# A graph network's last group of edges: nine columns instead of fourteen, and one pacing wait fewer

## The chip, the cores and the metric

The kernel runs on one core of a Trainium2 chip. The metric is the device time of one execution in microseconds (us). The core has five engines that work side by side, each with its own queue of instructions: TensorE (PE in the profile; PEld is its weight load), VectorE (DVE), ScalarE (ACT), GpSimd (POOL) and SyncE (SP). [...]data comes from device memory by DMA. The timed runs of the kernel before have a median of 8327.35 us (three runs, 8295.38 to 8355.8).

## The reference

There are 12500 nodes with 256 features each and 200000 edges, sorted by their destination node. Three graph layers are followed by one attention layer:

```
for each of three layers:                       # relu after the first two
    agg  = segment_sum(h[src], dst)             # sum over the incoming edges
    h    = h @ W_self + (agg / degree) @ W_neigh + b
x = layernorm(x + h)

zu = x @ U                                      # 4 heads of 16 numbers per node
logit = (zu[src] * zu[dst]).sum(-1) / 4         # per edge and head
alpha = softmax of logit over the edges of one destination
agg   = segment_sum(alpha * zu[src], dst)
half  = 0.5 * x + 0.5 * (head-weighted agg @ U^T)
x     = layernorm(x + relu(half + 0.5 * (half - half D^T D) D - 0.05))
```

Only the attention layer, the second block, is touched by the change at its heart. The matrices behind `half` are folded into two constants beforehand (`gz`, `gu`), so that per node only two products remain.

## The kernel before, in words

**Groups of edges.** The edges are cut into groups of `GE` = 128 x 14 = 1792. In a group, partition p holds 14 consecutive edges (`GT` = 14), one to a column. There are `NG` = 112 groups, numbered 0 to 111; the last has only 200000 - 111 x 1792 = 1088 edges. Laid fourteen to a partition they fill 77 partitions and 10 places of the next; what is left of the last group's 1792 places holds the destination `PAD` and the source 0. Because the edges are sorted, a group's destinations lie in a window of at most 128 nodes, that starts at the group's first destination (`starts`), or at node 12372 for the last groups, so that the window stays inside the table. `rel` is an edge's destination counted from the start of its group's window; a padded place lies far outside of it. All this is made once at the start (lines 187 to 279), from `srcI` and `dstI`, which are loaded at lines 198 to 202: all groups but the last by one transfer, the last by two more, on the queues of SP (dst) and ScalarE (src). The three layers (`fast_sage`) work through the groups up to a cut and do the remaining nodes in another way, so the last group is gathered in the attention alone.

**The attention** (`fast_attention`) takes the groups in turn. For each group:

1. SP loads rows of the window's 128 nodes, and `rel_d`, one row of 128 numbers per column, spread over all partitions (line 983), from which ScalarE makes `ohT`, a one-hot matrix from nodes to edges (lines 994 and 995).
2. GpSimd gathers the source rows of `zu_d` into `zs`, one indirect transfer of 128 rows per column, fourteen per group (lines 986 to 992, recorded at the helper's line 120).
3. VectorE makes `oh`, the one-hot matrix from edges to nodes (line 458).
4. In two halves of seven columns (`H` = 7), TensorE spreads the destination rows over the edges (`pD`, line 1006), VectorE multiplies by the gathered rows and sums (`zz`, `lg`, lines 1014 and 1017), ScalarE takes the exponential (1020) and copies it into the PSUM tile (1022), and both make the weighted rows `w` as a high and a low part (`wf`, `w`, lines 1023 to 1027).
5. TensorE sums `w` over the edges by node (`pA`, line 1030), with a product more that carries the sums of the group before into the new window (`carry`, line 465).
6. The sums are made into means (`acc`, `den`, `ag`, lines 1040 and 385 to 388), turned (`pT`, line 1044), multiplied (`pO`, lines 377 and 378), normalized (lines 402 to 403 and 333 to 338) and stored by SP (436).

**The order of the work.** `group` is a generator with five stages, and a loop starts one group and moves the four groups before it on by a stage. TensorE's order is written out: `in_order` chains every product to the one before it. In a round it has `pD` of group g, `pO` of g-3, `pT` of g-2 and `pA` of g-1. On the other engines a scheduler sets the order when the program is built, and each engine then works its queue off from the front. Two waits pace the gathers (`hold_back`): the first gather of a group waits for the products `pD` of the group before, and the eighth (`j == H`) waits for the sums `pA` of the group two before:

```
if j == 0 and g:
    hold_back(shown[-1], i)
if j == H and g > 1:
    hold_back(summed[g - 2], i)
```

Of the kernel before, what the change touches and what calls it, by code (L numbers as in the profile page):

```python
# [9 lines left out]
F32 = mybir.dt.float32  # L10
F32R = mybir.dt.float32r
# [5 lines left out]
AF = mybir.ActivationFunctionType  # L17
OP = mybir.AluOpType
# [5 lines left out]
P = 128  # L24
NB = 125
TE = 125
GT = 14
GE = P * GT
# [4 lines left out]
ND = 32  # L33
NDL = (16, 32, 32)
SG0, SG = 4, 8
# [13 lines left out]
def tile_gnn_resnorm(  # L49
# [13 lines left out]
    nc = tc.nc  # L63
    N, D = x.shape
    E = src.shape[0]
    K, _, R = u.shape
    KR = K * R
    DC = D // P
    NBLK = N // NB
    NG = -(-E // GE)  # L70
    L = len(w_self)
    AW = KR + K
    N0 = N - ND * P
# [4 lines left out]
    NU = ND // SG0  # L78
    U0 = NU - NDL[0] // SG0
# [18 lines left out]
            self.GS = (E * (self.n0 - P) // N - SLACK) // GE + 1  # L98
    cuts = {nd: Cut(nd) for nd in NDL}
    assert NQ % CB == 0 and NQ % ZB == 0 and NC * NQ < 512 and N0 % NC == 0 and SL == P == SG0 * P // NC  # L100
    assert NDL[0] % SG0 == 0 and 0 < U0 < NU and L == len(NDL) == 3 and NDL[1] == NDL[2] == ND and ND % SG == 0
    assert all(0 < c.GS < c.NGS < NG for c in cuts.values())
    assert N % NB == 0 and E % TE == 0 and D == 2 * P and KR == 64 and N + P < PAD and L > 1

# [10 lines left out]
    rel_d = dram.tile([NG * GT, P], F32, name="rel_d")  # L115
# [27 lines left out]
    npidx = const.tile([P, 1], F32, name="npidx")  # L143
# [43 lines left out]
    with tc.tile_pool(name="prep", bufs=1) as prep, \  # L187
# [3 lines left out]
        nc.vector.memset(dstI[:, NG - 1], PAD)  # L191
        nc.vector.memset(srcI[:, NG - 1], 0)
        last = (NG - 1) * GE
        full, rest = divmod(E - last, GT)
        EC = E // TE
        dall = prep.tile([TE, EC + SL], I32, name="dall")
        nc.vector.memset(dall[:, EC:], PAD)
        for t, ap, q in ((dstI, dst, nc.sync), (srcI, src, nc.scalar)):
            q.dma_start(t[:, :NG - 1], ap[:last].rearrange("(g p j) -> p g j", p=P, j=GT))
            q.dma_start(t[:full, NG - 1], ap[last:last + full * GT].rearrange("(p j) -> p j", j=GT))  # L200
            if rest:
                q.dma_start(t[full:full + 1, NG - 1, :rest], ap[E - rest:][None, :])
        nc.sync.dma_start(dall[:, :EC], dst.rearrange("(p j) -> p j", p=TE))
# [248 lines left out]
        nc.vector.tensor_copy(c, iota[:, :n])  # L452
        return c

    def onehot(wk, nodes, r, dt=F32, name="oh", op=OP.is_equal, bufs=2):

        oh = wk.tile([P, GT, P], dt, name=name, bufs=bufs)
        nc.vector.tensor_tensor(oh, r.unsqueeze(2).to_broadcast([P, GT, P]),  # L458
                                nodes.unsqueeze(1).to_broadcast([P, GT, P]), op=op)
        return oh  # L460

    def carry(wk, pa, d, before):
# [496 lines left out]
    def fast_attention():  # L959
        loads[0] = None  # L960
        H = GT // 2
        with tc.tile_pool(name="att", bufs=2) as wk, \
                tc.tile_pool(name="att_c", bufs=1, space=PSUM) as cps, \
                tc.tile_pool(name="att_ps", bufs=1, space=PSUM) as ps:
            nodes = group_consts(cps)
            order, sums = [None], [None]
            shown, summed = [], []

            def in_order(first, last):
                if order[0] is not None:  # L970
                    after(order[0], first)
                order[0] = last

            def group(g):

                zb = wk.tile([P, D], F32, name="zb", bufs=8)
                zT = wk.tile([P, DC, P], F32, name="zT", bufs=6)
                zn = wk.tile([P, KR], F32, name="zn", bufs=3)
                load_rows([(zn, zu_d), (zb, z_d), (zT, zt_d)], g)

                ohT = wk.tile([P, GT, P], F32R, name="ohT", bufs=3)
                rT = ohT.bitcast(F32).rearrange("p j e -> p (j e)")
                nc.sync.dma_start(rT, rel_d[g * GT:(g + 1) * GT, :].rearrange("j e -> (j e)")[None, :]
                                  .to_broadcast([P, GT * P]))
                zs = wk.tile([P, GT, KR], F32, name="zs", bufs=6)
                for j in range(GT):
                    i = gather(zs[:, j], zu_d, srcI[:, g, j:j + 1])

                    if j == 0 and g:
                        hold_back(shown[-1], i)  # L990
                    if j == H and g > 1:
                        hold_back(summed[g - 2], i)
                oh = onehot(wk, nodes, rel[:, g], F32R, bufs=3)
                nc.scalar.activation(ohT.rearrange("p j e -> p (j e)"), rT, AF.Abs, bias=npidx)
                nc.scalar.activation(ohT.rearrange("p j e -> p (j e)"), rT, AF.Relu, scale=-1.0, bias=1.0)

                z2 = wk.tile([P, K, 2, R], F32R, name="z2", bufs=3)
                zk = zn.rearrange("p (k r) -> p k r", r=R)
                nc.scalar.activation(z2[:, :, 0], zk, AF.Copy)
                nc.vector.tensor_tensor(z2[:, :, 1], zk, z2.bitcast(F32)[:, :, 0], op=OP.subtract)  # L1000

                w = wk.tile([P, GT, 2 * AW], F32R, name="w", bufs=3)
                for a in (0, H):

                    pd = ps.tile([P, (H + 1) * 2 * KR], F32, name="pD", bufs=2)
                    mm = [nc.tensor.matmul(pd[:, j * 2 * KR:(j + 1) * 2 * KR], ohT[:, a + j],  # L1006
                                           z2.rearrange("p k i r -> p (k i r)"), start=True, stop=True)
                          for j in range(H)]
                    in_order(mm[0], mm[-1])
                    shown.append(mm[-1])  # L1010

                    zg = zs[:, a:a + H].rearrange("p t (k r) -> p (t k) r", r=R)
                    zz = wk.tile([P, H * K, 2, R], F32, name="zz")
                    nc.vector.tensor_mul(zz, zg.unsqueeze(2).to_broadcast([P, H * K, 2, R]),  # L1014
                                         pd[:, :H * 2 * KR].rearrange("p (m i r) -> p m i r", i=2, r=R))
                    lg = wk.tile([P, H, K], F32, name="lg")
                    nc.vector.reduce_sum(lg.rearrange("p t k -> p (t k)"), zz.rearrange("p m i r -> p m (i r)"),  # L1017
                                         axis=AX.X)
                    wf = wk.tile([P, H, AW], F32, name="wf")
                    nc.scalar.activation(wf[:, :, KR:], lg, AF.Exp, scale=0.25)  # L1020
                    pe = pd[:, H * 2 * KR:H * (2 * KR + K)].rearrange("p (t k) -> p t k", k=K)
                    nc.scalar.activation(pe, wf[:, :, KR:], AF.Copy)
                    nc.vector.tensor_mul(wf[:, :, :KR].rearrange("p t (k r) -> p t k r", r=R),  # L1023
                                         zs[:, a:a + H].rearrange("p t (k r) -> p t k r", r=R),
                                         pe.unsqueeze(3).to_broadcast([P, H, K, R]))
                    nc.scalar.activation(w[:, a:a + H, :AW], wf, AF.Copy)
                    nc.vector.tensor_tensor(w[:, a:a + H, AW:], wf, w.bitcast(F32)[:, a:a + H, :AW], op=OP.subtract)  # L1027
                yield
                pa = ps.tile([P, 2 * AW], F32, name="pA")
                mm = [nc.tensor.matmul(pa, oh[:, j], w[:, j], start=j == 0, stop=g == 0 and j == GT - 1)  # L1030
                      for j in range(GT)]
                if g:
                    mm.append(carry(wk, pa[:, :AW], delta[:, g:g + 1], sums[0]))
                in_order(mm[0], mm[-1])
                summed.append(mm[-1])
                yield
                part = wk.tile([P, AW], F32, name="part")
                nc.scalar.activation(part, pa[:, AW:2 * AW], AF.Copy)
                acc = wk.tile([P, AW], F32, name="acc", bufs=3)
                nc.vector.tensor_add(acc, part, pa[:, :AW])  # L1040
                sums[0] = acc
                ag = attention_mean(wk, acc, 1e-30, OP.max)
                pt = ps.tile([P, P], F32, name="pT")
                mm = nc.tensor.transpose(pt[:KR], ag, ident)  # L1044
                in_order(mm, mm)
                yield
                agT = attention_turned(wk, pt, P)
                pg, *mm = gradient_step(ps, zT, agT)
                in_order(*mm)
                yield  # L1050
                o, made = attention_end(wk, zb, pg)
                store_rows([(o, out)], g, made)
                yield

            live = []
            for g in range(NG + 4):
                if g < NG:
                    live.append(group(g))  # L1060
                    next(live[-1])
                old = live[:-1] if g < NG else live
                for s in old:
                    next(s)
                if g >= 4:
                    live.pop(0)
            assert not live
# [204 lines left out]
```

## Time and profile before

| what | us |
|---|---|
| timed runs: median (lowest, highest) | 8327.35 (8295.38, 8355.8) |
| the profiled execution, as timed | 6588.12 |
| its span, from the first to the last instruction | 6586.3 |
| TensorE busy (share of the span) | 5115.1 (78%) |
| GpSimd busy | 4862.9 (74%) |
| VectorE busy | 3948.0 (60%) |
| ScalarE busy | 3431.3 (52%) |
| gathers of `zs` in the attention: 1568, busy | 1504.8 |
| mean granted clock of TensorE | 0.810 |

The profile is of one execution, and all its durations belong to that one, whose time stands in the second row; the timed runs are longer. A line of the page's groups names the source line, the engine, the tile written and the tiles read, and the count; then the busy time and the mean duration of one, and the idle time of the engine just before, with what ended it. In a listing in order of time the first number is the start, the second the duration, and the bracket at the end says how long the engine had been idle and what released it. The chain that ended last is followed back from the last instruction, at each step to what released it.

### The profile page before, as it was taken

The page shows a single profiled execution, that of the slowest core. Times are in us where ns is not written, and L with a number is a line of the kernel's source. Part 1 is how long each engine was busy: PE and PEld are TensorE (multiplying, and loading weights), DVE is VectorE, ACT ScalarE, POOL GpSimd, SP SyncE. Part 2 cuts the span into 40 slices and gives each one's busy share as a digit, 9 for nine tenths or more (in the row PEclk, how much of TensorE's full clock was granted, in tenths as well). Part 3 has the DMA queues.
Part 4 walks back from the last instruction along what each step waited for, and adds up shares of the span by engine and source line. Part 5 has one row for each costly group of instructions (what it writes and reads, how often), then busy time and mean ns, then how long its engine had stood idle before and what let it go on. Part 6 is the DMA issues. An engine that isn't in the chain of part 4 may idle for free. (4 is left out here: it accounts for less than half of the span.)

```text
span 6586.3 us, 86342 instructions
## 1 busy us (share of the span) xinstructions
PE 5115.1 (78%) x23316; PEld 4174.4 (63%) x23316; DVE 3948.0 (60%) x10037; ACT 3431.3 (52%) x6215; POOL 4862.9 (74%) x5038
## 2 busy tenths in 40 slices
PE   5778888788799999998899999995455555555555
PEld 3566666677577777776678888884444444444444
DVE  5778776455454555555556666666566555556655
ACT  2434444555466666665456666663455545545554
POOL 6767777777677777777677777774777777777775
PEclk8889999899899999999999999997555555555555
DMA  8967777888677888886788888884333333333332
GB/s 231 319 214 254 259 239 265 269 297 294 210 248 254 272 263 270 265 270 211 230 253 264 269 269 270 267 261 128 98 100 101 106 101 100 103 105 100 101 107 66
DMA packets 878807, 1367.35 MB, mean 208 GB/s; under 512 B 191090, under 2 KB 533130, under 8 KB 874207
## 3 DMA queue, kind: packets, MB, share of 16 engines
q1 hardware_dynamic: 629744, 802.71, 36.6%
q0 software_dynamic: 216000, 504.16, 25.6%
q10 hardware_dynamic: 32559, 54.81, 2.5%
q8 instruction: 187, 3.06, 0.2%
q14 instruction: 317, 2.60, 0.1%
HBM read 1150.87 MB, written 210.33 MB: 207 GB/s over the span
## 5 line engine op out<-in xcount | busy, mean ns | idle before, releaser
L120 POOL DMA_INDIRECT xg<-h_d,srcI x2128 | 2067.9, 972 | 696.5 <-issue 304.2
L750 PE MATMUL px<-c,hz 128*128 128x512 f32 x7840 | 2153.6, 414 | 102.3 <-ACT c L744 73.0
L120 POOL DMA_INDIRECT zs<-zu_d,srcI x1568 | 1504.8, 960 | 547.8 <-issue 434.3
L750 PEld LDWEIGHTS px<-c,hz 128*128 128x128 f32 x7840 | 1457.5, 192 | 402.0 <-ACT c L744 90.7
L120 POOL DMA_INDIRECT xg<-in_x_dram,srcI x1274 | 1228.7, 964 | 429.7 <-issue 159.0
L744 ACT ACTIVATE c<-c 128x1024 fp32r<-128x1024 uint8 (+1 forms) x1176 | 1063.0, 914 | 696.2 <-PE px L750 548.5
L850 DVE TENSOR_TENSOR hl<-xg,hl 128x256 fp32r<-128x256 f32 x2128 | 790.5, 420 | 529.3 <-ACT hl L848 506.6
L458 DVE TENSOR_TENSOR oh<-rel,gconst 128x1792 fp32r<-128x1792 f32 (+1 forms) x358 | 722.7, 2019 | 364.2 <-PE pA L856 228.1
L848 ACT ACTIVATE hl<-xg 128x512 fp32r<-128x512 f32 x1216 | 646.3, 571 | 529.1 <-DMA xg<-h_d,srcI 399.7
L1044 PE MATMUL pT<-ident,ag 128*64 128x128 f32 x112 | 47.3, 422 | 894.4 <-DVE ag L388 894.4
L1044 PEld LDWEIGHTS pT<-ident,ag 128*64 128x64 f32 x112 | 14.5, 129 | 974.2 <-DVE ag L388 972.2
L1014 DVE TENSOR_TENSOR zz<-zs,pD 128x896 f32<-128x896 f32 x224 | 242.8, 1084 | 637.5 <-DMA zs<-zu_d,srcI 633.5
L856 PE MATMUL pA<-hl,oh 128*128 128x512 f32 x2128 | 583.0, 409 | 10.9 <-DVE hl L850 8.1
L864 PE MATMUL pA<-xg,oh 128*128 128x258 f32 x1764 | 457.9, 410 | 21.4 <-DMA xg<-in_x_dram,srcI 16.8
L856 PEld LDWEIGHTS pA<-hl,oh 128*128 128x128 f32 x2128 | 406.8, 193 | 106.6 <-DVE hl L850 13.5
L641 ACT ACTIVATE win<-pc 128x392 uint16<-128x392 f32 x512 | 242.0, 500 | 359.6 <-PE pc L638 335.0
L864 PEld LDWEIGHTS pA<-xg,oh 128*128 128x128 f32 x1764 | 350.2, 206 | 90.9 <-DMA xg<-in_x_dram,srcI 26.2
L1006 PE MATMUL pD<-z,ohT 128*128 128x128 f32 x1568 | 361.8, 418 | 38.5 <-DVE wf L1023 20.1
L1006 PEld LDWEIGHTS pD<-z,ohT 128*128 128x128 f32 x1568 | 348.0, 334 | 39.2 <-DVE wf L1023 20.5
L1030 PE MATMUL pA<-w,oh 128*128 128x136 f32 x1568 | 362.3, 419 | 0.0
L1020 ACT ACTIVATE wf<-lg 128x28 f32<-128x28 f32 x224 | 50.6, 226 | 583.0 <-DVE lg L1017 581.8
L630 DVE TENSOR_SCALAR ob<-iota,kt 128x196 bf16<-128x196 f16 x1024 | 349.3, 344 | 0.0
(254 smaller groups left out, 8002.1 us busy)
## 6 DMA issues: line engine op xcount, KB each, us to landing
hz<-hs_d SPq DMA_DIRECT2D x588, 512.0 KB
c<-cnt_d SPq DMA_DIRECT2D x112, 896.0 KB
ohT<-rel_d SPq DMA_DIRECT2D x112, 896.0 KB
hs_d<-hs SPq DMA_DIRECT2D x218, 256.0 KB
cnt_d<-win ACTq DMA_DIRECT2D x32, 1568.0 KB
xg<-h_d,srcI POOLq DMA_INDIRECT x2128
c<-cnt_d SPq DMA_DIRECT2D x56, 448.0 KB
zs<-zu_d,srcI POOLq DMA_INDIRECT x1568
```

What stands on the lines that cost most here:

```text
L120: return nc.gpsimd.indirect_dma_start(out=dst_ap, out_offset=None, in_=table, in_offset=bass.IndirectOffsetOnAxis(ap=idx, axis=0))
L458: nc.vector.tensor_tensor(oh, r.unsqueeze(2).to_broadcast([P, GT, P]), nodes.unsqueeze(1).to_broadcast([P, GT, P]), op=op)
L630: nc.vector.tensor_scalar(ob[:, c], iota16[:, 1:1 + NQ * 2], kt[:, 1, at], kt[:, 2, at], op0=OP.is_equal, op1=OP.mult)
L744: nc.scalar.activation(c32.rearrange("p (k d) -> p k d", d=P), c8[:, :, b % CB], AF.Copy)
L750: made.append(nc.tensor.matmul(px[f][i], hz[:, b % ZB, a:a + P].bitcast(F32R), c32[:, i * 512:(i + 1) * 512], start=b == 0 and part == 0, ...
L848: nc.scalar.activation(hi[:, b + j:b + j + n, :W], xg[:, a + j:a + j + n, :W], AF.Copy)
L850: nc.vector.tensor_tensor(lo[:, b + j, :D], xg[:, a + j, :D], hf[:, b + j, :D], op=OP.subtract)
L856: mm.append(nc.tensor.matmul(pa, oh[:, a + j], hl[:, j].rearrange("p i d -> p (i d)"), start=first, stop=stop))
L864: mm.append(nc.tensor.matmul(pa[:, :W], oh[:, a + j], xg[:, a + j, :W], start=first, stop=stop))
L1006: mm = [nc.tensor.matmul(pd[:, j * 2 * KR:(j + 1) * 2 * KR], ohT[:, a + j], z2.rearrange("p k i r -> p (k i r)"), start=True, stop=True) f ...
L1014: nc.vector.tensor_mul(zz, zg.unsqueeze(2).to_broadcast([P, H * K, 2, R]), pd[:, :H * 2 * KR].rearrange("p (m i r) -> p m i r", i=2, r=R))
L1030: mm = [nc.tensor.matmul(pa, oh[:, j], w[:, j], start=j == 0, stop=g == 0 and j == GT - 1) for j in range(GT)]
```

## The change

For the last group alone, the edges are laid nine to a partition: `LT` is the number of columns that 1088 edges need over 128 partitions, which is 9. They fill 120 partitions and 8 places of the next. Everything that the attention does per column is done for `T` columns, where `T` is 14, and 9 for the last group: nine gathers, a one-hot matrix of nine columns on either side, halves of seven and two columns, nine products `pD` and nine `pA`. The arrays keep their sizes; the columns 9 to 13 of the last group hold padding. The eighth gather of the last group (`j == H`) is no longer held back; that of all other groups is, as before. Cut to its core:

```
+    LT = -(-(E - (NG - 1) * GE) // P)
...
-        full, rest = divmod(E - last, GT)
+        full, rest = divmod(E - last, LT)
...
-            q.dma_start(t[:full, NG - 1], ap[last:last + full * GT].rearrange("(p j) -> p j", j=GT))
+            q.dma_start(t[:full, NG - 1, :LT], ap[last:last + full * LT].rearrange("(p j) -> p j", j=LT))
...
-    def onehot(wk, nodes, r, dt=F32, name="oh", op=OP.is_equal, bufs=2):
+    def onehot(wk, nodes, r, dt=F32, name="oh", op=OP.is_equal, bufs=2, m=GT):
...
-        nc.vector.tensor_tensor(oh, r.unsqueeze(2).to_broadcast([P, GT, P]),
-                                nodes.unsqueeze(1).to_broadcast([P, GT, P]), op=op)
+        nc.vector.tensor_tensor(oh[:, :m], r[:, :m].unsqueeze(2).to_broadcast([P, m, P]),
+                                nodes.unsqueeze(1).to_broadcast([P, m, P]), op=op)
...
+                T = GT if g < NG - 1 else LT
...
-                rT = ohT.bitcast(F32).rearrange("p j e -> p (j e)")
-                nc.sync.dma_start(rT, rel_d[g * GT:(g + 1) * GT, :].rearrange("j e -> (j e)")[None, :]
-                                  .to_broadcast([P, GT * P]))
+                rT = ohT.bitcast(F32)[:, :T].rearrange("p j e -> p (j e)")
+                nc.sync.dma_start(rT, rel_d[g * GT:g * GT + T, :].rearrange("j e -> (j e)")[None, :]
+                                  .to_broadcast([P, T * P]))
...
-                for j in range(GT):
+                for j in range(T):
...
-                    if j == H and g > 1:
+                    if j == H and 1 < g < NG - 1:
                         hold_back(summed[g - 2], i)
-                oh = onehot(wk, nodes, rel[:, g], F32R, bufs=3)
+                oh = onehot(wk, nodes, rel[:, g], F32R, bufs=3, m=T)
...
-                for a in (0, H):
+                for a, n in ((0, H), (H, T - H)):
...
-                mm = [nc.tensor.matmul(pa, oh[:, j], w[:, j], start=j == 0, stop=g == 0 and j == GT - 1)
-                      for j in range(GT)]
+                mm = [nc.tensor.matmul(pa, oh[:, j], w[:, j], start=j == 0, stop=g == 0 and j == T - 1)
+                      for j in range(T)]
```

Within a half, every operation on `H` columns becomes one on `n` columns: `zz`, `lg`, `wf`, the copy into the PSUM tile, and both parts of `w`.

More of the change, by code (lines that the diff above doesn't have):

```diff
@@ L100, in tile_gnn_resnorm @@
     assert NQ % CB == 0 and NQ % ZB == 0 and NC * NQ < 512 and N0 % NC == 0 and SL == P == SG0 * P // NC
-    assert NDL[0] % SG0 == 0 and 0 < U0 < NU and L == len(NDL) == 3 and NDL[1] == NDL[2] == ND and ND % SG == 0
+    assert NDL[0] % SG0 == 0 and 0 < U0 < NU and L == len(NDL) == 3 and NDL[1] == NDL[2] == ND and ND % SG == 0 and GT // 2 < LT <= GT
     assert all(0 < c.GS < c.NGS < NG for c in cuts.values())
@@ L990, in group @@
                         hold_back(shown[-1], i)
-                    if j == H and g > 1:
+                    if j == H and 1 < g < NG - 1:
                         hold_back(summed[g - 2], i)
-                oh = onehot(wk, nodes, rel[:, g], F32R, bufs=3)
-                nc.scalar.activation(ohT.rearrange("p j e -> p (j e)"), rT, AF.Abs, bias=npidx)
-                nc.scalar.activation(ohT.rearrange("p j e -> p (j e)"), rT, AF.Relu, scale=-1.0, bias=1.0)
+                oh = onehot(wk, nodes, rel[:, g], F32R, bufs=3, m=T)
+                oT = ohT[:, :T].rearrange("p j e -> p (j e)")
+                nc.scalar.activation(oT, rT, AF.Abs, bias=npidx)
+                nc.scalar.activation(oT, rT, AF.Relu, scale=-1.0, bias=1.0)
                 z2 = wk.tile([P, K, 2, R], F32R, name="z2", bufs=3)
@@ L1007, in group @@
                                            z2.rearrange("p k i r -> p (k i r)"), start=True, stop=True)
-                          for j in range(H)]
+                          for j in range(n)]
                     in_order(mm[0], mm[-1])
                     shown.append(mm[-1])
[L1012 to L1015, printed above, removed]
@@ L1016, in group @@
-                    lg = wk.tile([P, H, K], F32, name="lg")
+                    zg = zs[:, a:a + n].rearrange("p t (k r) -> p (t k) r", r=R)
+                    zz = wk.tile([P, H * K, 2, R], F32, name="zz")[:, :n * K]
+                    nc.vector.tensor_mul(zz, zg.unsqueeze(2).to_broadcast([P, n * K, 2, R]),
+                                         pd[:, :n * 2 * KR].rearrange("p (m i r) -> p m i r", i=2, r=R))
+                    lg = wk.tile([P, H, K], F32, name="lg")[:, :n]
                     nc.vector.reduce_sum(lg.rearrange("p t k -> p (t k)"), zz.rearrange("p m i r -> p m (i r)"),
@@ L1018, in group @@
                                          axis=AX.X)
-                    wf = wk.tile([P, H, AW], F32, name="wf")
+                    wf = wk.tile([P, H, AW], F32, name="wf")[:, :n]
                     nc.scalar.activation(wf[:, :, KR:], lg, AF.Exp, scale=0.25)
-                    pe = pd[:, H * 2 * KR:H * (2 * KR + K)].rearrange("p (t k) -> p t k", k=K)
+                    pe = pd[:, H * 2 * KR:H * 2 * KR + n * K].rearrange("p (t k) -> p t k", k=K)
                     nc.scalar.activation(pe, wf[:, :, KR:], AF.Copy)
@@ L1023, in group @@
                     nc.vector.tensor_mul(wf[:, :, :KR].rearrange("p t (k r) -> p t k r", r=R),
[L1024 to L1027, printed above, removed]
+                                         zs[:, a:a + n].rearrange("p t (k r) -> p t k r", r=R),
@@ L1028, in group @@
+                                         pe.unsqueeze(3).to_broadcast([P, n, K, R]))
+                    nc.scalar.activation(w[:, a:a + n, :AW], wf, AF.Copy)
+                    nc.vector.tensor_tensor(w[:, a:a + n, AW:], wf, w.bitcast(F32)[:, a:a + n, :AW], op=OP.subtract)
                 yield
                 pa = ps.tile([P, 2 * AW], F32, name="pA")
-                mm = [nc.tensor.matmul(pa, oh[:, j], w[:, j], start=j == 0, stop=g == 0 and j == GT - 1)
-                      for j in range(GT)]
+                mm = [nc.tensor.matmul(pa, oh[:, j], w[:, j], start=j == 0, stop=g == 0 and j == T - 1)
+                      for j in range(T)]
```

## The prediction

> **What bounds the kernel now.** I read the page's busy times and slices first, then the groups of the attention stage, then the chain that ended last over the final 65 us, and last the instructions in order of time there.
>
> ```profile
> PE 5115.1 (78%) x23316; PEld 4174.4 (63%) x23316; DVE 3948.0 (60%) x10037; ACT 3431.3 (52%) x6215; POOL 4862.9 (74%) x5038
> ...
> POOL 6767777777677777777677777774777777777775
> PEclk8889999899899999999999999997555555555555
> ```
>
> The first line is the whole kernel, and settles nothing: two stages share it, as the clock in the last line shows. The busy times by stretch give the split: the layers run to about 4440 us with TensorE 77% to 95% busy, the attention takes the last 2146 us. There GpSimd is the steady engine, as its group of gathers between 5000 and 6480 us shows (busy us, mean ns, idle us before them):
>
> ```profile
> L120 POOL DMA_INDIRECT zs<-zu_d,srcI x1170 | 1124.5, 961 | 356.6 <-issue 323.7 <-DMA zs<-zu_d,srcI 32.3 <-PE pO L378 0.6
> ```
>
> That is 1.27 us from start to start, hardly ever held by anything but issue, and fourteen make a round of 17.7 us. So the stage goes at the pace of the gathers, and only its end can go differently.
>
> The chain that ended last (start, us, what), its end:
>
> ```profile
> 6543.94 2.40 DMA zs<-zu_d,srcI
> 6546.52 1.09 DVE zz L1014
> ...
> 6547.87 0.99 DVE lg L1017
> ...
> 6551.73 0.42 PE pT L1044
> 6552.15 2.89 PE pA L1030 x14
> 6555.03 0.43 PE pA L465 x2
> 6555.46 2.98 PE pD L1006 x14
> ...
> 6561.40 0.35 PE pT L1044
> ...
> 6568.38 2.89 PE pA L1030 x14
> ...
> 6580.64 0.41 DVE g L338
> ```
>
> One gather, issued at 6543.94, sets zz, and through VectorE's queue the mean ag and its transpose pT; from 6551.73 TensorE runs almost without a gap to the last products. The gathers there, in order of time:
>
> ```profile
> 6542.70 0.94 POOL L120 DMA_INDIRECT zs<-zu_d,srcI  x1 [0.30 <-issue]
> 6543.94 0.94 POOL L120 DMA_INDIRECT zs<-zu_d,srcI  x1 [0.30 <-PE pO L378]
> 6545.19 0.95 POOL L120 DMA_INDIRECT zs<-zu_d,srcI  x1 [0.30 <-issue]
> 6555.73 0.94 POOL L120 DMA_INDIRECT zs<-zu_d,srcI  x1 [9.59 <-PE pA L465]
> ```
>
> Here the built program's order is needed. The scheduler doesn't leave a held gather in its place: GpSimd's queue has the twelve unheld gathers of group g, then the eighth of group g-1, then the first of g. So the twelve of group 111 (the last) start from 6528.71 to 6542.70; 6543.94 is the eighth of group 110; 6545.19 is the first of 111; and 6555.73, after 9.59 us, is the eighth of 111, held by the sums of group 109. VectorE beside it:
>
> ```profile
> 6546.52 1.09 DVE L1014 TENSOR_TENSOR zz<-zs,pD 128x896 f32<-128x896 f32 x1 [4.89 <-DMA zs<-zu_d,srcI]
> 6551.45 0.22 DVE L388 TENSOR_TENSOR ag<-acc,den 128x64 f32<-128x64 f32 x1
> ...
> 6558.11 1.09 DVE L1017 TENSOR_REDUCE lg<-zz 128x28 f32<-128x896 f32 x1
> 6559.11 1.08 DVE L1014 TENSOR_TENSOR zz<-zs,pD 128x896 f32<-128x896 f32 x1
> ```
>
> zz of 110's second half waits 4.89 us for the gather of 6543.94. zz of 111's second half (6559.11) shows no idle at all: the gather that waited 9.59 us is not late for anyone.
>
> [...]0.94 us on GpSimd, but 2.40 us in the chain before zz may go. [...]The trace has the 1283 ns[...] (a load at 6541.71 has its exponential at 6543.00). [...]
>
> **The change part by part.** On every engine the program is the same up to the last rounds of the attention, apart from four loads at the start.
>
> *The loads (L200, L202).* 120 pieces of 36 bytes instead of 77 of 56, in each of two queues. The issue of L200 on SP shows 20.98 us behind L199's 14208 pieces, some 1.5 ns each: 43 more are 0.06 us. Above, a whole microsecond could be lost if short pieces cost 20 times that; below, nothing, since there are more pieces. VectorE first needs dstI at 26.76 us, while GpSimd gathers without pause from 3.85. I take 0. Without that cover it is 0.06 to 1 us. SP's later dall loads, queued behind, move by the same.
>
> *Five gathers fewer.* The last group issues nine. Eight (seven, and the eighth gather, now unheld) stand ahead of 110's eighth instead of twelve: 4 x 1.25 = 5.0 us, so it starts at 6538.95. Its own hold, the sums of 108, is over at 6537.87 (the carry L465 of that round starts at 6537.24), so the slot is kept, with 1.1 us to spare. It lands 2.4 us later, 6541.4. The first gather of 111 follows at 6540.20, or at 6541.1 once the products pD of 110 (to 6540.85) are done; needed near 6549, it has cover.
>
> *VectorE's queue before it.* oh of 111 starts at 6537.48 and has 1152 instead of 1792 elements: 1.36 for 2.02 us, to 6538.84. acc and sh (0.5 us) now go first, then 110's first zz at 6539.4, which needs seven pD products (6537.87 + 1.49 = 6539.36), and its reduction from 6540.6. So 110's second zz starts at 6541.6, for 6546.52.
>
> *ag moves up.* In the new order ag of 108 follows directly on the second reduction; before, it stood behind two wf and two w. zz 6541.6, reduction 6542.8, ag 6543.8 to 6544.0, where it ended at 6551.67: **7.6 us sooner**. TensorE is done with pO at 6543.82, so pT and pA of 109 follow at once; w of 109 has long been there. That ends the cover: next late is TensorE.
>
> *TensorE's share.* The last group's pD are nine, not fourteen: 5 x 2.98/14 = **1.1 us** less; pA likewise 5 x 2.89/14 = **1.0 us**. Both lie in the unbroken stretch.
>
> *A new wait.* pD of 111 ends at 6549.85, pO of 108 at 6552.8, and pT of 109 could go. But ag of 109 now stands in VectorE's queue behind g of 108 (L403), which waits for the Relu after that pO (0.55 us later in the trace: 6561.40 to 6561.95), and behind bn_st. So 6553.35 + 0.42 + 0.17 + 0.43 + 0.22 = 6554.6: **1.8 us** lost, with pA of 110 and everything behind pT on TensorE waiting. Bounds: 0, if the two engines overlap otherwise, to 3.
>
> *ScalarE.* The square-root table load now comes between the exponentials of 111 and their copies. Relu 6552.85, loads and exponentials to 6556.35, bn_rs and copies to 6557.0, wf, w on both engines to 6559.1. pT of 110 is due 6.6 us after pT of 109, 6561.2, and pA of 111 after it: 2.1 us of cover. I take 0[...]. The Abs on ohT (1.24 for 1.77 us) and the shorter zz, lg, wf, w lie beside TensorE's stretch: 0, at most 1 gained.
>
> *The pacing wait itself.* 0: its gather was late for nobody.
>
> Sum: -7.6 - 1.1 + 1.8 - 1.0 = **-7.9 us**. The profiled execution took 6588.1 us (6586.3 of span and 1.8 around it), so 6580.2. The three timed runs lie at 8327.35, 1.264 times that. Nothing in the profile says where those 1739 us lie. If none is in the tail, the gain is 7.9; if all stretches grow alike, 10.0. I take 9.3: **8318 us**.
>
> **The rivals.**
> *The cut stays hidden.* If ScalarE or the old order binds, the 7.6 are lost, and 2.1 remain: 8325. For it, VectorE has little room between 6539 and 6544; against it, the 4.89 us idle that names the gather. 0.14.
> *The wait was what held.* A reader of the waits would add its 9.59 us to five gathers of 1.25: 15.8 us, 8310. Against it stands zz at 6559.11 without idle. With it goes the case that the new wait of 1.8 us doesn't come (-9.7). 0.16.
> *Slower[...].* The place is the table load ahead of the copies of 111. It decides once the stretch from Relu to w takes over 2.1 us more, and ends above the old time once it takes 2.1 + 7.9 = 10 us more, 5 for each of its two table loads. At 12 more it is +2: 8329. The trace's 1283 ns speaks against it. 0.04.
> The forecast itself, a gain of 6 to 9 us in the profile: 0.66.
>
> **How the numbers follow.** All four lie within 0.2% of each other; a measurement of this kernel tells about 1% (83 us) from no change. The times shown spread 60 us over three runs, more than any case moves, so scatter makes the range. The rivals' gains on the lowest run give 8280 and on the highest 8357; three runs understate a spread, and both medians carry it, so I add 15 us on each side, rounded: 8265 to 8372. Over 1% either way needs scatter beyond anything shown: 0.05 faster, 0.04 slower, 0.91 within.
>
> **What would show it.** In the profile after: 110's second zz near 6541.6 with little or no idle; pT of 108 near 6544.1; no GpSimd wait near 10 us; pT of 109 with about 1.8 us of idle before it, released by ag; a span near 6578. If that idle is missing, the new wait was wrong; if zz still waits 4 us or more, the queue's order was. A change of over 20 us in the span would mean that something before the last rounds moved, and the whole reading would be wrong.

## The result, and the profile after

The kernel after takes 8339.38 us (median of 22 runs, 8287.14 to 8394.53), the kernel before, measured beside it, 8347.15 us (22 runs, 8276.94 to 8391.6). The ratio of after to before is put at 1.0004, with a 95% interval of 0.9985 to 1.0024 (the two medians alone give 0.9991): no difference that can be told. The interval is some 33 us wide, four times the 7.9 us that the working arrived at, so this number alone neither confirms nor refutes a single step, and every rival of the prediction would have passed by it too.

The profile can, with one caution. All timed runs of both kernels took 8205 to 8395 us, and so did the profiled execution of after (8334.37 us); the one profile of before that the prediction was made from, 6588.1 us, was of a shorter kind of execution that was not met again. For a fair comparison the unchanged kernel was profiled once more:

> The whole kernel before, one look, for a profile of the long kind of execution (about 8340 us, as the timed runs and the profile of after) in place of the one of 6588 us. If the forecast's steps hold in that kind too, the step between the transposes of the 107th and 108th groups is 18 to 21 us here against 9.77 us in after, the step 108 to 109 is 9.6 us, the steps 109 to 110 and 110 to 111 are 6.6 us each, and from the transpose of the 107th to the end it is 52 to 54 us against 43.8. The rival, that the earlier transpose is a trait of the long kind of execution and not of the change, has the step 107 to 108 below 12 us here too.

It took 8325.86 us. The pages of the two, busy time and slices, first before and then after:

```profile
PE 5508.9 (66%) x23316; PEld 4394.3 (53%) x23316; DVE 3945.0 (47%) x10037; ACT 3419.7 (41%) x6215; POOL 4876.3 (59%) x5038
...
POOL 5555555555556665566555555654366666666665
```

```profile
PE 5506.2 (66%) x23306; PEld 4391.4 (53%) x23306; DVE 3938.3 (47%) x10037; ACT 3415.5 (41%) x6215; POOL 4852.7 (58%) x5033
...
POOL 6555555555466665656455555554366666666665
```

GpSimd has five instructions fewer (5033 for 5038) and TensorE ten (five products pD, five pA); the busy times of all engines agree within 0.5%. The 1738 us that separate the longer profile of before from the first one are a matter of the kind of execution, not of the change.

What the change did is seen in the last rounds. The transpose `pT` is issued once per group, so the times between its starts, read from the instructions in order of time, cut the tail into rounds (us):

| step of pT, groups | before, 6588 us | before, again | after |
|---|---|---|---|
| 106 to 107 | 18.28 | 17.92 | 23.62 |
| 107 to 108 | 17.60 | 20.95 | **9.77** |
| 108 to 109 | 9.61 | 9.61 | **10.22** |
| 109 to 110 | 6.62 | 6.62 | 6.62 |
| 110 to 111 | 6.62 | 6.62 | **5.55** |
| sum | 58.7 | 61.7 | 55.8 |

From the transpose of 107 to the end it is 55.6 us in before again, somewhat more than the 52 to 54 expected, and 43.8 us in after.

The instructions of after in order of time, round of 108 (start, us, engine, line, what; the bracket is the idle time before and what ended it):

```profile
8286.48 0.94 POOL L121 DMA_INDIRECT zs<-zu_d,srcI  x1 [0.30 <-issue]
...
8292.13 1.35 DVE L459 TENSOR_TENSOR oh<-rel,gconst 128x1152 fp32r<-128x1152 f32 x1 [1.87 <-PE pA L1033]
...
8292.79 0.94 POOL L121 DMA_INDIRECT zs<-zu_d,srcI  x1 [5.37 <-PE pA L466]
...
8294.04 1.09 DVE L1017 TENSOR_TENSOR zz<-zs,pD 128x896 f32<-128x896 f32 x1 [0.23 <-PE pD L1009]
...
8296.17 1.08 DVE L1017 TENSOR_TENSOR zz<-zs,pD 128x896 f32<-128x896 f32 x1
...
8298.29 0.22 DVE L389 TENSOR_TENSOR ag<-acc,den 128x64 f32<-128x64 f32 x1
...
8298.56 0.42 PE L1047 MATMUL pT<-ident,ag 128*64 128x128 f32 x1
```

GpSimd's unheld gathers of the last group now end at 8287.42, 5.4 us before the eighth gather of group 110 (8292.79), and what that gather waits for is its own pacing wait on the sums of 108, not the queue. The second `zz` of 110 (8296.17) has no idle before it, where the first profile had 4.89 us until the gather landed. `ag` follows directly on its reduction.

### The profile page after: what moved, and what is told of

The parts are those of the page before. It is cut to its first block, busy times and chain, and to the rows that moved or that the text cites. A ratio compares the mean times of both kernels' runs of the same rounds, so it can differ in the third digit from the quotient of the medians.

```text
span 8332.6 us, 86317 instructions
## 1 busy us (share of the span) xinstructions
PE 5506.2 (66%) x23306; PEld 4391.4 (53%) x23306; DVE 3938.3 (47%) x10037; ACT 3415.5 (41%) x6215; POOL 4852.7 (58%) x5033
## 5 line engine op out<-in xcount | busy, mean ns | idle before, releaser
L751 PE MATMUL px<-c,hz 128*128 128x512 f32 x7840 | 2326.8, 437 | 283.8 <-ACT c L745 119.2
L751 PEld LDWEIGHTS px<-c,hz 128*128 128x128 f32 x7840 | 1554.9, 205 | 666.4 <-issue 187.8
L849 ACT ACTIVATE hl<-xg 128x512 fp32r<-128x512 f32 x1216 | 621.1, 568 | 317.5 <-PE pA L857 84.1
L857 PE MATMUL pA<-hl,oh 128*128 128x512 f32 x2128 | 622.0, 427 | 68.1 <-issue 66.1
L865 PE MATMUL pA<-xg,oh 128*128 128x258 f32 x1764 | 518.9, 452 | 9.4 <-issue 4.4
L857 PEld LDWEIGHTS pA<-hl,oh 128*128 128x128 f32 x2128 | 428.4, 204 | 178.0 <-issue 77.3
L865 PEld LDWEIGHTS pA<-xg,oh 128*128 128x128 f32 x1764 | 399.2, 233 | 100.3 <-issue 16.2
L639 PE MATMUL pc<-ob,oa 128*128 128x196 bf16 x1024 | 193.1, 272 | 371.5 <-ACT win L642 115.2
L344 DVE TENSOR_TENSOR pO<-b,pO 128x256 f32<-128x256 f32 x306 | 130.3, 426 | 639.9 <-remote 469.4
L354 PE MATMUL pO<-ws,hT 128*128 128x256 f32 x984 | 285.3, 416 | 133.2 <-DVE hs L658 49.3
```

The costliest lines, as they stand in the source:

```text
L354: mm = [nc.tensor.matmul(po, hT[:, i], wts[i // DC][:, i % DC], start=i == 0, stop=i == 2 * DC - 1) for i in range(2 * DC)]
L751: made.append(nc.tensor.matmul(px[f][i], hz[:, b % ZB, a:a + P].bitcast(F32R), c32[:, i * 512:(i + 1) * 512], start=b == 0 and part == 0, ...
L849: nc.scalar.activation(hi[:, b + j:b + j + n, :W], xg[:, a + j:a + j + n, :W], AF.Copy)
L857: mm.append(nc.tensor.matmul(pa, oh[:, a + j], hl[:, j].rearrange("p i d -> p (i d)"), start=first, stop=stop))
L865: mm.append(nc.tensor.matmul(pa[:, :W], oh[:, a + j], xg[:, a + j, :W], start=first, stop=stop))
```

## The experiments

The gain looked for is a thousandth of the run, and a run of the whole kernel scatters by more. So a *short form* of each kernel was made: the layers are left out, the attention's tables are filled from the input, and only groups 96 to 111 are worked. On the last rounds the engines' queues are in the same order as in the whole kernel. It takes about 460 us and its repeats agree to a few us. All runs named "short" below are of this form; "short before" and "short after" are those of the two kernels.

**1 and 2. The change in short form.**

> A short form of the kernel before: the three layers are left out, the attention's tables are filled from x instead, and the attention does groups 96 to 111 alone, in the same order and with the same waits; its output isn't the reference's. It is the base for the other short forms. All theories: some 300 to 450 us; the last rounds look as in the long kernel (the last gather waits about 9.6 us, TensorE then works without a gap), and from the start of pA of group 108 to the last instruction about 47 us.

> The short form of the changed kernel. My theory: 7.9 us less than the short form of before (6 to 9.7). Rival, the cut stays hidden: 2.1 us less. Rival, the wait was what held: 15.8 us less. Slower rival: more than the short form of before.

Before: 465.94 us (median of five, 465.27 to 467.8). After: 457.88 us (452.39 to 458.15). The difference is **-8.06 us**, where the sum had -7.9. The steps, as in the table above: before 18.80, 20.26, 9.61, 6.62, 6.62; after 22.23, 9.80, 10.22, 6.62, 5.55. The two profiled executions differ by 9.8 us. The five steps make 7.5 of them, and 2.3 stand in the rounds before, where the two programs are the same. So the agreement of -8.06 with -7.9 is closer than the scatter of the runs would lead one to expect, and in part luck. The base itself took longer than the 300 to 450 us expected of it. From the start of `pA` of 108 to its end it has 52.9 us, not 47 (the profile of 6588 us has 52.1), and its last gather waits 10.08 us.

**3 and 4. The pacing wait by itself.** Taken away from before, with fourteen columns kept:

```
-                    if j == H and g > 1:
+                    if j == H and 1 < g < NG - 1:
```

> The short form of before, fourteen columns in every group, with the pacing wait of the last group's eighth gather left out and nothing else. My theory: that gather now stands in GpSimd's queue ahead of 110's eighth, which starts 1.25 us later, so 0 to 1.5 us more than the short form of before. Rival, the wait was what held: 9.6 us less.

and put back into after, with nine columns kept (the same lines, exchanged):

> The short form of the changed kernel, nine columns, with the pacing wait of the last group's eighth gather put back. My theory: 110's eighth gather starts another 1.25 us earlier, which VectorE can't use, and 111's eighth lands some 0.3 us late: within 1.5 us of the short form of the changed kernel, so 6 to 9 us under the short form of before. Rival, the wait was what held: it loses 9.6 us against the short form of the changed kernel.

The first gave 467.16 us (466.93 to 469.1), 1.2 us more than short before; the second 458.49 us (457.31 to 461.42, six runs), 0.6 us more than short after. Neither change is near the 9.6 us of the rival. In the second, the instructions in order of time show why (GpSimd's held gather, then the two `zz` of the last group):

```profile
431.14 0.94 POOL L123 DMA_INDIRECT zs<-zu_d,srcI  x1 [5.85 <-PE pA L468]
...
432.39 1.09 DVE L1035 TENSOR_TENSOR zz<-zs,pD 128x896 f32<-128x896 f32 x1 [0.53 <-PE pD L1027]
...
433.69 0.42 DVE L1035 TENSOR_TENSOR zz<-zs,pD 128x256 f32<-128x256 f32 x1 [0.20 <-DMA zs<-zu_d,srcI]
```

The gather waits 5.85 us, and its user stands idle 0.20 us for it. The wait in the queue was long, and hardly anything needed its end.

**5. The five gathers by themselves.** Short after, with fourteen gathers in the last group again; the five fill columns that nothing reads, and all other engines keep nine:

```
-                for j in range(T):
+                for j in range(GT):
                     i = gather(zs[:, j], zu_d, srcI[:, g, j:j + 1])
```

> The short form of the changed kernel (layers left out, the attention's tables filled from the input, groups 96 to 111 only) with one edit: the last group again issues fourteen gathers, the five of them past its nine columns fetching rows that nothing reads. TensorE's, VectorE's and ScalarE's work on the last group stays at nine, and there is no pacing wait. If the gain comes from the gathers that no longer stand in GpSimd's queue ahead of the 110th group's eighth (my theory), the step between the transposes of the 107th and 108th groups goes back from 9.8 to 19 to 20.5 us, the step before it falls from 22.2 to about 19, and the whole takes 464 to 466 us, at most 2 us less than the short form of before (465.94). If the gain is from the smaller work of the other engines, or from the changed order on VectorE, it stays at 457 to 459 us.

464.46 us (460.37 to 467.51), against 458.29 us (453.8 to 458.87) of short after on the same chip. The ranges don't overlap. In the traces of the two, TensorE, VectorE and ScalarE have their last rounds in the same order, operation by operation. So **6.2 of the 8 us** go with nothing but five gathers in a queue. (Without the pacing wait, one gather more stands ahead of 110's eighth than in before; experiment 3 puts that at 1.2 us, within the scatter.) Its profile has the steps 19.89, 19.42, 10.22, 6.10, 3.56, and this in the round of 108 (instructions in order of time):

```profile
424.00 0.94 POOL L123 DMA_INDIRECT zs<-zu_d,srcI  x1 [0.30 <-issue]
...
427.61 0.47 ACT L405 ACTIVATE g<-pO,shrink 128x256 f32<-128x256 f32 x1 [3.38 <-remote]
427.74 0.94 POOL L123 DMA_INDIRECT zs<-zu_d,srcI  x1 [2.80 <-remote]
...
428.14 1.09 DVE L1035 TENSOR_TENSOR zz<-zs,pD 128x896 f32<-128x896 f32 x1 [5.51 <-DMA zs<-zu_d,srcI]
...
430.27 0.22 DVE L391 TENSOR_TENSOR ag<-acc,den 128x64 f32<-128x64 f32 x1
```

The step 107 to 108 is back at 19.4 us, and `zz` again waits 5.51 us until 110's eighth gather (424.00) has landed. But it is not the picture of the first profile. There `zz` went 2.58 us after that gather's start, here 4.14 us after it; and ScalarE's Relu (427.61) and GpSimd's next gather (427.74), which wait for TensorE and not for this gather, were released only some 0.5 us before `zz`. The last two steps are short for another reason: in this execution TensorE ran the last nine `pA` in 1.20 us instead of 2.17, and the next four products of `pO` (448.17) in 1.08 us instead of 2.01. With short after's last two steps in their place the sum of the five steps is 61.7 us, against 61.9 of short before.

**6. The new wait by itself.** Short after with one order given: the addition `g` of group 108 goes behind the mean `ag` of 109 in VectorE's queue (`first` is that mean's last operation, given for group 108 alone). With it, the scheduler also moved ScalarE's `agT` of 109 and two copies ahead of a table load.

```
-        nc.vector.tensor_mul(ag.rearrange("p (k r) -> p k r", r=R),
+        averaged.append(nc.vector.tensor_mul(ag.rearrange("p (k r) -> p k r", r=R),
...
-        nc.vector.tensor_add(g, zz, g)
+        i = nc.vector.tensor_add(g, zz, g)
+        if first is not None:
+            after(first, i)
```

> The short form of the changed kernel with one edit: on VectorE the mean ag of the 109th group is put ahead of the addition g of the 108th, so that the transpose of the 109th no longer waits for ScalarE's Relu of the 108th and VectorE's addition. If the new wait that I put at 1.8 us (1.61 us of idle time on TensorE in the trace of after) lies on the path to the end, this takes 1.3 to 2.0 us less than the short form of after, 456 to 456.6 us against 457.9, and the step 108 to 109 falls from 10.22 to about 8.6 us. The rival says that the wait is covered by something that comes as late (the 109th's second product, or TensorE's late signals): within 0.5 us of the short form of after, the step 109 to 110 growing by what the step 108 to 109 loses.

> The short form of the changed kernel once more, as the measure for the two runs beside it on the same chip: 457.3 to 458.5 us.

456.96 us (456.47 to 458.06) against 458.29: 1.3 us less in the median, though the ranges overlap. The trace is plain. Without the order, short after has the same wait as the whole changed kernel, which shows:

```profile
8307.71 0.42 DVE L404 TENSOR_TENSOR g<-zb,g 128x256 f32<-128x256 f32 x1 [1.08 <-ACT g L403]
...
8308.51 0.21 DVE L389 TENSOR_TENSOR ag<-acc,den 128x64 f32<-128x64 f32 x1
...
8308.78 0.42 PE L1047 MATMUL pT<-ident,ag 128*64 128x128 f32 x1 [1.61 <-DVE ag L389]
```

With the order given, the short form has

```profile
433.76 0.22 DVE L393 TENSOR_TENSOR ag<-acc,den 128x64 f32<-128x64 f32 x1
...
434.04 0.42 PE L1069 MATMUL pT<-ident,ag 128*64 128x128 f32 x1
...
434.60 0.43 DVE L408 TENSOR_TENSOR g<-zb,g 128x256 f32<-128x256 f32 x1 [0.61 <-ACT g L407]
```

The transpose of 109 has no idle before it, the step 108 to 109 is 8.60 us for 10.22, and the steps after it are unchanged, so the 1.62 us lie on the path to the end. (In that one execution the two steps before were 1.4 us longer than in the repeat of short after, which is their scatter.)

**7. That order in the whole kernel.**

> The whole changed kernel with the order on VectorE as in the short form with ag of the 109th group ahead of g of the 108th. 1.3 to 1.6 us less than after, which runs of a whole kernel can't tell: within 0.4% of before. In its profile the step between the transposes of the 108th and 109th groups is 8.6 us in place of 10.22, and the 109th's transpose has no wait near 1.6 us for VectorE's ag.

8242.67 us (20 runs, 8183.59 to 8279.58), before beside it 8238.16 us; ratio 1.0001, interval 0.9981 to 1.002. Nothing to be told, as expected; the step 108 to 109 is 8.60 us here too. By the traces it is the better order, by 1.6 us.

**8 and 9. What sets the longer round.** In the profile that the prediction rests on, a round of the attention is 17.7 us, the pace of fourteen gathers. In every later profile with all its gathers and products it is 20.1 to 20.5 us in the mean, and other engines then wait on TensorE long after its products' recorded ends (in before again ScalarE's `part` of 108 starts 7.7 us after them). Two short forms asked on which side that hangs. One replaces the second half of the gathers by a plain load of other rows:

```
+                nc.sync.dma_start(zs[:, H:T], bass.AP(x.tensor, 0, [[GT * KR, P], [KR, T - H], [1, KR]]))
-                for j in range(T):
+                for j in range(H):
```

> The short form of the changed kernel, with the second half of every group's gathers (and the pacing wait with them) replaced by one plain load of other rows, so that GpSimd issues seven gathers a group in place of fourteen. The question is what sets the round of 20.2 us that every timed execution shows, against 17.6 us in the profiled execution of before. If it is GpSimd's queue, the rounds fall to 9 to 13 us (seven gathers at 1.25 us are 8.8 us). If it is the chain of TensorE's results and their late signals, the rounds stay at 16 to 20 us and the whole falls by at most 50 us from 458.

the other forms `pA` from seven columns and leaves the others out:

```
-                      for j in range(T)]
+                      for j in (*range(H - 1), T - 1)]
```

> The short form of the changed kernel, with pA formed from seven of a group's columns in place of fourteen (the others are left out), so that TensorE has some 1.6 us less of 9.2 us of work in a round; the gathers stay at fourteen. If TensorE's share of work sets how late its signals come[...], the rounds fall in proportion, from 20.2 to about 17.6 us, where the gathers hold them, and the whole falls by 25 to 35 us from 458. If TensorE's work has no part in it, the rounds stay at 19.8 to 20.3 us and the whole falls by under 10 us, or with them only the 1.6 us by which the products are shorter, 12 times, some 19 us.

Both ran on another chip than the forms above. With seven gathers: 369.19 us (367.65 to 369.5), rounds of 12.6 us. The fall by 89 us is much more than the 50 us at most of its second theory, and the rounds lie in the range of the first. With seven products: 452.01 us (450.15 to 453.06), some 6 us less than short after, where rounds in proportion to the work would have given 25 to 35 us less; the rounds scatter between 17.8 and 22.8 us with a mean of 19.9. So a sixth less work on TensorE does not shorten the round in proportion, and its amount of work is not what sets it. ScalarE's waits in short after and with seven gathers, both between 210 and 300 us (engine, line, what it waited for: us in total, times, longest):

```profile
ACT part L1059 <- remote: 21.2, 3, 7.3
ACT z L1020 <- remote: 9.5, 4, 3.4
...
ACT part L1059 <- PE pO L381: 5.5, 1, 5.5
```

```profile
ACT z L1021 <- PE pD L1028: 13.8, 6, 3.1
ACT g L405 <- PE pO L381: 4.5, 7, 1.2
```

`part` only needs the sums `pA`, and in short after it waits up to 7.3 us for a release that the trace can't name ("remote"). With seven gathers that wait is gone. The edit also takes the eighth gather's pacing wait away and adds a plain load, so it shows that the late releases go with the gathers, not by which way.

How the longer round comes about can be read from GpSimd's own waits. In before again, between 7900 and 8200 us (14.8 rounds), it has (us in total, times, longest):

```profile
POOL zs L120 <- PE pO L378: 38.7, 14, 3.1
```

About once a round a gather held by a pacing wait stands 2.8 us for TensorE. With fourteen gathers at 1.25 us, 17.5 us, that makes 20.3 us. In the profile of 6588 us such waits are 0.6 us in all between 5000 and 6480 us, as the prediction's line of the gathers shows. Whether the rounds would shrink without the pacing waits was not tried.

## Why the prediction held, point by point

The prediction was right: the forecast of no difference that can be told is what came, and the median of 8339.38 lies inside the range. That much needed no more than the scatter. Its steps can be judged on the short forms and the traces.

**Five gathers fewer, and `ag` moves up (-7.6 us): near in size, right in that the gathers are the cause, but mostly not by the path described.** The step 107 to 108 fell further than put down, by 10.5 us in short form (20.26 to 9.80) where 7.6 were taken off. The step before it grew, by 3.4 us (18.80 to 22.23); together -7.0 us, and -5.5 us between the two whole profiles of the longer kind. That growth was not foreseen. The chain that ended last of after shows it (start, us, what):

```profile
8276.13 0.23 ACT wf L1023
8276.35 8.95 another core or an unknown queue
8285.32 0.48 ACT g L403
8285.92 1.16 DVE wf L1026 x2
8287.08 1.71 issue
8288.79 0.42 PE pT L1047
```

ScalarE stands idle for 8.95 us before its Relu (L403), which waits for a product `pO` whose records end at 8274.84; the copies behind it in ScalarE's queue, then `wf`, `w` and `ag` of 107 on VectorE come late with it. In the 6588 us execution the Relu's waits on `pO` between 4700 and 6500 us were 1.2 us at the longest.

The picture of *how* a long queue of gathers holds the round is also not the same in this kind of execution. In the repeat of before the second `zz` of 110 has no idle; what was late is everything that TensorE releases:

```profile
8277.11 0.95 POOL L120 DMA_INDIRECT zs<-zu_d,srcI  x1 [0.30 <-issue]
8279.99 0.23 ACT L1038 ACTIVATE part<-pA 128x68 f32<-128x68 f32 x1 [10.46 <-remote]
8280.23 0.95 POOL L120 DMA_INDIRECT zs<-zu_d,srcI  x1 [2.17 <-remote]
8282.16 1.09 DVE L1014 TENSOR_TENSOR zz<-zs,pD 128x896 f32<-128x896 f32 x1 [4.36 <-remote]
```

`part` of 108, whose products' records end at 8272.3, comes at 8279.99, 1.9 us after GpSimd's unheld gathers end (8278.06). In after they end at 8287.42, before those products, and `oh` and `part` are released as these are done. The short forms with fourteen gathers in the last group agree: in short before, the first `zz` of 110 stands 5.11 us for a release called "remote" and the second has no idle; in experiment 3 it is 5.05 and 0.67 us, both "remote". Among these only experiment 5 has a wait for the gather, and there TensorE's releases came almost as late. So five gathers fewer help either way: by the landing of one gather, as argued, or by ending sooner the time in which TensorE's releases are late. The prediction named the first; experiment 5 shows that the gathers are the cause, and experiment 8 that late releases go with them. That the second is what happens in most executions is a reading of these traces, not shown by an edit. That a path which these executions don't take came out near the measured gain is in part luck.

**TensorE's share (-1.1 and -1.0 us): right.** The step 110 to 111 went from 6.62 to 5.55 us (-1.07). The nine pD took 2.16 us for 3.23 in the trace (-1.07), and with the new wait removed the step 108 to 109 is 8.60 us against 9.61 (-1.01).

**A new wait (+1.8 us): right.** The trace has 1.61 us of idle before the transpose of 109, released by `ag` behind `g`, and experiment 6 gets 1.62 back.

**The pacing wait (0): right.** Experiments 3 and 4 put its removal at +1.2 and -0.6 us, in fourteen and in nine columns: no gain beyond the scatter, and not the 9.6 of the rival. The prediction had 110's eighth gather reach its slot with its own pacing wait over for 1.1 us. In the longer kind of execution it waits 5.37 us there, and still its `zz` waits for nothing.

**ScalarE (0): right.** A table load takes in after what it took in before, 1.28 us, and the exponential follows at once: a load at 8296.61 has its exponential at 8297.91. The step 110 to 111, in which `pA` of 111 runs, is shorter by the five products and no more (5.55 us for 6.62), so ScalarE's part of the last group came in time. The rival that made ScalarE the slowest falls; that a table load would cost more than its 1.28 us was an assumption of the author's, which no trace of this case shows. The two durations that the author put down for shapes which the profile of before doesn't show came in: `oh` of 1152 elements, put at 1.36 us, took 1.35, and the Abs on `ohT` of 1152 elements, put at 1.24, took 1.24.

**The loads at the start (0)** were not tried alone. The short forms contain them, and their first transpose starts at 181.0 and 180.5 us in the two with the loads of before, and at 180.3 to 181.0 us in the five with those of after and all gathers and products: no microsecond is seen, but the scatter is nearly as large.

**From 7.9 to 9.3 us.** The stretch by the ratio of the two kinds of execution was a wrong step: the last rounds didn't grow with the rest. The steps 9.61, 6.62, 6.62 are equal to the hundredth in executions of 6588 and 8326 us. Of the 1738 us between these, 1458 come before the attention's first transpose (at 4631.98 and 6089.81 us; in after at 6098.5) and 280 in the rounds that follow it, up to the last three steps. The unscaled sum, -7.9, was the better number for a measured -8.06.

**The span near 6578 us** was not seen, because the profiled execution was of the other kind. The other marks were seen: 110's second `zz` without idle, no wait of GpSimd near 10 us, 1.6 us before the transpose of 109. The first of them is no sign of the change in the longer kind of execution, since before again has it too.

## What to carry to other kernels

A wait that stands long in the profile says nothing of its worth; look at the first user of what it holds back. Here 9.59 us of pacing were worth nothing, and five gathers that nothing waited for, but that stood in a queue ahead of others, were worth 6 us. When work leaves one queue, go through the order of the others as well: in the new program the mean `ag` of 109 came to stand behind an addition of the group before, and that cost 1.6 us. A path read from one profile may not be the path of the next execution, so profile again before trusting it. And a gain of a thousandth is measured in a short form that has only the stage concerned, not in the whole kernel.

## What the runs showed of the hardware that was not expected

The same program ran in two kinds of execution, of 6588 and of about 8330 us, with equal durations of instructions in the tail (fourteen `pA` 3.23 us, a `zz` 1.09, a gather 0.94 to 0.95 on GpSimd, in the 6588 us profile and in before again). In the longer kind, engines that wait for TensorE in the attention were released several us after the products' recorded ends (10.5 us for after's Relu at 8285.32; 7.7 us for `part` of 108 in before again, before which ScalarE stood idle for 10.46 us, put down to "remote"), and a round takes 20.3 us instead of 17.7. With seven gathers in place of fourteen ScalarE's long waits are gone (rounds of 12.6 us; between 210 and 300 us its longest wait for TensorE is 3.1 us, in short after 7.3 by "remote"); with half of `pA`'s products the long round stays (mean 19.9 us). The granted clock does not tell the two kinds apart there: it is 0.50 in the attention's steady rounds of the 6588 us profile (5000 to 6480 us) and of after (6200 to 8270 us). Why the profile of 6588 us shows fourteen gathers a round without it, at the same pace of 1.25 us from gather to gather, stays open, and so does whether the time lost in the layers has the same cause.
